# Which taps of a convolution go to which engine, in a fused state-space and attention kernel: the last chunk of four, the place of an eviction, and a clamp through PSUM

## The chip, the cores and the metric

The kernel runs on one core of one Trainium2 chip. The time is the device time of one execution in microseconds; times of several runs are given as median and range. A profile is one execution taken by the hardware profiler: start and end of the instructions of each engine, what released a waiting instruction, the DMA packets and the granted TensorE clock. The engines are called PE (TensorE), DVE (VectorE), ACT (ScalarE), POOL (GpSimd) and SP (SyncE, which here only issues DMAs).

## What is computed

Two layers on x of shape (2, 768, 64, 64). The change touches only the first, a two-dimensional Mamba block:

```python
x = hs @ in_proj_w.T                                  # 768 -> 1536 channels
xs = depthwise 3x3 convolution of x, + conv_b
xs = xs * sigmoid(xs)
dt, Bs, Cs = split(xs_seq @ x_proj_w.T, [R, R + DSTATE])
delta = softplus(dt @ dt_w + dt_b)
dA = exp(delta * A);  dBu = delta * u * Bs            # 4 states
states = associative scan of s = dA * s + dBu along the 4096 tokens
y = sum over states(states * Cs) + D * u
var = y.var(-1)
y = (y - mean) * rsqrt(var + 1e-5) * ln_g + ln_b      # over the 1536 channels
out = y @ out_proj_w.T                                # 1536 -> 768
```

A group norm stands before it and x is added to its output. The second layer (group norm, a token-statistics attention with two 768 x 768 products, residual) follows in the same program.

## The kernel before

**Tiles and steps.** The 2 x 4096 tokens are cut into 16 tiles of 512 tokens (8 image rows). The 1536 channels are 12 chunks of 128, so there are 192 pairs of tile and chunk, and the program is a sequence of steps g with three stages at different distances: the convolution runs ahead on chunk a = g + 15 (`AHEAD`, line 52), its input product on chunk n = g + 17, the scan works on chunk g, and the output product trails by 12 (`BEHIND`, line 53). Steps before g = 0 only fill this pipeline: 17 of them, after the group norm's statistics have been taken from a first reading of x. Every engine carries out its instructions in the order in which `step` (line 921) writes them; there is no reordering. Four chunks form a rhythm: the silu of chunks a-4 to a-1 runs in the steps with g % 4 = 1, followed by their x_proj products, and one third of a tile's output is evicted in steps with g % 4 = 0.

**The nine taps of the convolution.** `tap_act` (384) writes the centre tap into the PSUM tile acc on ACT. The other eight are divided by two tables, `DMA_TAPS` and `PE_TAPS` (lines 48 and 49, indexed by a % 4; `FILL_TAPS` for a < 15):
- A PE tap is a matmul with a diagonal matrix that adds into acc. ACT makes the diagonal (`diag`, 377); `taps_pe` (414) stands in the step before the chunk's own, behind that step's out_proj.
- A DMA tap is a scaled shifted copy made by ACT (`taps_act`, 393, tile tm), which DMAs with accumulation, issued by POOL, add up: `taps_dma_sum` (403) into the first tm, then `taps_dma` (408) into the chunk's result u.
- All remaining taps are DVE instructions (`taps_dve`, 423), one after the other on acc, the last one writing u.

For a chunk with three DMA taps (`late_tap`, line 1016) the second sum is issued in the chunk's own step and the final one is moved to the end of POOL's DMAs of that step; with two taps the final one stands ahead of the next chunk's first sum.

**One step on each engine.** DVE: the taps of chunk a, every fourth step the eviction of two output tiles (`out_evict`, 574: po times rs), then the scan's product s (506), the scan (508) and the product with C (515, tile da). In every twelfth step (g % 12 = 3) the layer norm's variance follows (`norm_rs2`, 551), from which ACT makes rs with Ln and Exp. POOL: `sum1` of the chunk before (493, tile ysum), `du` (485), then DMAs: tap sums, two y sums (501), and every fourth step the residual x (583). ACT: silu or softplus with their table loads, centre tap, eviction of in_proj (355), scaled copies for DMA taps, exps (480). PE: in_proj (342), norm sums, out_proj (558), PE taps, x_proj. SP issues the loads; behind g % 12 = 11 it broadcasts B and C of the next tile to all partitions (`load_bc`, 463).

**The fill.** In steps 8 to 15 of the fill the output weights are scaled by ln_g on ACT and their mean is subtracted on POOL (`out_weights_scale`, 274), behind the rest of the step; the table `ready_w` says which of the 12 blocks come in which step, one or two at a time. The in_proj results use one PSUM bank (psA), output products a pair of banks (psO) that the fill needs only for the weights' mean.

Of the kernel before, what the change touches and what calls it, by code (L numbers as in the profile page):

```python
# [7 lines left out]
F32 = mybir.dt.float32  # L8
AF = mybir.ActivationFunctionType
ALU = mybir.AluOpType  # L10
# [4 lines left out]
P = 128  # L15
# [7 lines left out]
KI = DI // P  # L23
# [11 lines left out]
NQ0 = NI * KI  # L35
# [9 lines left out]

DMA_TAPS = ((0, 2, 6), (0, 2), (0, 2, 6), (0, 2, 6))
PE_TAPS = ((), (1,), (), (1,))
FILL_TAPS = (0, 2)  # L50

AHEAD = 15
BEHIND = 12
# [13 lines left out]
def both_layers(  # L67
# [43 lines left out]
    def take():  # L111
        return slots.pop(0)
# [9 lines left out]
    def give_w(w):  # L122
        wst.append(w.rearrange("p k m -> p (k m)"))
    wk = ctx.enter_context(tc.tile_pool(name="l0wk", bufs=2))
    psA = ctx.enter_context(tc.tile_pool(name="l0_psa", bufs=1, space=PSUM))
# [3 lines left out]
    psO = ctx.enter_context(tc.tile_pool(name="l0_pso", bufs=1, space=PSUM))  # L129
# [121 lines left out]
    def out_weights_rows(wg, rows):  # L251
        gb = psO.tile([P, 2, 512], F32, tag="po", name="pgb")
        for k in range(KI):
            for j in range(KM // 2):
                nc.tensor.matmul(
                    gb[32 * j : 32 * j + 2, 0, :MG], pc[:, k, PC_G : PC_B + 1], wg[:, k, j * MG : (j + 1) * MG],
                    start=(k == 0), stop=(k == KI - 1),
                )
        for j in range(KM // 2):
            nc.scalar.copy(rows[32 * j : 32 * j + 2, :], gb[32 * j : 32 * j + 2, 0, :MG])  # L260

    def out_weights_mean(rows, wmean, pick):
        pb = psS.tile([P, 512], F32, tag="st", name="pbo")
        wm = psO.tile([P, 2, 512], F32, tag="po", name="pwm")
        for j in range(KM // 2):
            for e in range(2):
                m = 2 * j + e
                nc.tensor.matmul(pb[:, m : m + 1], rows[:, e * P : (e + 1) * P], pick[:, j, P : P + 1], start=True, stop=True)
            nc.tensor.matmul(wm[:, j // 2, j % 2 * MG : (j % 2 + 1) * MG], pick[:, j, :P], rows, start=True, stop=True)
        nc.scalar.copy(wmean[:, : 2 * MG], wm[:, 0, :])  # L270
        nc.scalar.copy(wmean[:, 2 * MG :], wm[:, 1, :MG])
        nc.scalar.copy(bias_o, pb[:, :KM])

    def out_weights_scale(wg, wmean, k):
        nc.scalar.activation(wg[:, k, :], wg[:, k, :], AF.Copy, scale=pc[:, k, PC_G : PC_G + 1])
        nc.gpsimd.tensor_sub(wg[:, k, :], wg[:, k, :], wmean)

    def out_weights_store(wg, k):
        nc.sync.dma_start(
# [6 lines left out]
    def where(n):  # L286
        i, c = divmod(n, KI)
        return i, c, i // NT, i % NT
# [53 lines left out]
    def in_proj(n):  # L342
        i, c, b, t = where(n)
        nn = TL if t < NT - 1 or b + 1 < NB else TL - W
        w = wis.pop(n)
        pa = psA.tile([P, 512], F32, tag="psa", name=f"pa{n}")
        for k in range(KM):
            nc.tensor.matmul(pa[:, :nn], w[:, k, :], xts[i, k][:, :nn], start=(k == 0), stop=(k == KM - 1))  # L348
        pas[n] = pa
        give_w(w)  # L350
        if c == KI - 1:
            for k in range(KM):
                give(xts.pop((i, k)))
# [15 lines left out]


    def dma_taps(a):
        return DMA_TAPS[a % 4] if a >= AHEAD else FILL_TAPS

    def pe_taps(a):
        return PE_TAPS[a % 4] if a >= AHEAD else ()

    def diag(a):
        c = a % KI
# [14 lines left out]
    def taps_act(a):  # L393
        xs, c = xs_bufs[a % 2], a % KI
        tms[a] = (tm_bufs[a % 2], tm_bufs[2], tm_bufs[3 + a % 2]) if a >= AHEAD else (take(), take())
        for tm, j in zip(tms[a], dma_taps(a)):
            dy, dx = divmod(j, 3)
            nc.scalar.activation(  # L398
                tm.rearrange("p (h w) -> p h w", w=W), xs[:, dy : dy + TR, dx : dx + W], AF.Copy,
                scale=pc[:, c, PC_W + j : PC_W + j + 1],  # L400
            )

    def taps_dma_sum(a, q):
        nc.gpsimd.dma_start(tms[a][0], tms[a][q], accum_op=ALU.add)  # L404
        if a < AHEAD:
            give(tms[a][q])

    def taps_dma(a):
        tm = tms.pop(a)[0]
        nc.gpsimd.dma_start(us[a], tm, accum_op=ALU.add)  # L410
        if a < AHEAD:
            give(tm)
# [7 lines left out]
                skip_group_check=True,  # L420
            )

    def taps_dve(a):
        c = a % KI
        taps = [j for j in range(9) if j != 4 and j not in pe_taps(a) + dma_taps(a)]
        xs, acc = xs_bufs[a % 2], accs.pop(a).rearrange("p (h w) -> p h w", w=W)
        u = take()
        us[a] = u
        for j in taps:
            dy, dx = divmod(j, 3)  # L430
            dst = u.rearrange("p (h w) -> p h w", w=W) if j == taps[-1] else acc
            nc.vector.scalar_tensor_tensor(  # L432
                dst, xs[:, dy : dy + TR, dx : dx + W], pc[:, c, PC_W + j : PC_W + j + 1], acc, ALU.mult, ALU.add
            )

    def silu(a):
        nc.scalar.activation(us[a], us[a], AF.Silu, bias=pc[:, a % KI, PC_CB : PC_CB + 1])
# [15 lines left out]
    def x_sum(i):  # L453
        px = psX.tile([P, 512], F32, tag="px", name=f"pxs{i}")
        nc.tensor.matmul(px[:XM, :], xsum, pxs["halves"], start=True, stop=True)
        give(pxs.pop("halves"))
        pxs["sum"] = px
# [43 lines left out]
    def y_dma(g, n):  # L501
        nc.gpsimd.dma_start(us[g], ysums(g, n), accum_op=ALU.add)  # L502
# [46 lines left out]
        return pm, mu2  # L549

    def norm_rs2(i, pm, mu2):
        nc.vector.scalar_tensor_tensor(mu2, mu2, -1.0, pm[:, 1, :], ALU.mult, ALU.add)
        nc.vector.tensor_scalar_max(mu2, mu2, 0.0)
        nc.scalar.activation(rs, mu2, AF.Ln, bias=eps_c)
        nc.scalar.activation(rs, rs, AF.Exp, scale=-0.5)

# [17 lines left out]
    def out_evict(g):  # L574

        po = pos[0]
        i, r = (g - 1 - BEHIND) // KI, (g - 1) % KI
        for e in range(2):
            xr = take()
            nc.vector.tensor_mul(xr, po[:, e, :], rs)  # L580
            xrs[i, 2 * (r // 4) + e] = xr
# [60 lines left out]
    def norm_x1(b, j, k):  # L642
        nc.scalar.activation(
            x1s[b, j, k], x1s[b, j, k], AF.Identity, bias=bias1[b][:, k : k + 1], scale=scale1[b][:, k : k + 1]
        )
# [248 lines left out]
    with tc.manual_schedule():  # L894
# [26 lines left out]
        def step(g, prep=None):  # L921
            a, n = g + AHEAD, g + AHEAD + 2
            v = n
# [29 lines left out]
                norms[g][0][1]()  # L953
            if xd_now:
                x_sum(g // KI + 1)
            if 0 <= a < NQ0:
                taps_dve(a)
            if BEHIND < g <= NQ0 + BEHIND and (g - BEHIND) % 4 == 0:
                out_evict(g)
            for q in by_step[v - 1] if 0 < v <= len(by_step) else ():  # L960
                gn_piece(1, q)
            if BEHIND + 2 < g and (g - BEHIND) % 4 == 2:
# [33 lines left out]
            elif n < NQ0 + N_TAIL:  # L996
# [3 lines left out]
                    load_x1(0, d[1] + 1, k)  # L1000
                for k in {3: [0], 4: [1], 5: [2, 3, 4, 5]}.get(d[2], []):
                    norm_x1(0, d[1] + 1, k)
            if 0 <= a + 1 < NQ0:
                taps_act(a + 1)
            if 0 <= g - 3 < NQ0:
                square(g - 3)
# [9 lines left out]
            late_tap = 0 <= a < NQ0 and len(dma_taps(a)) > 2  # L1016
# [3 lines left out]
                y_dma(g - 1, 0)  # L1020
            if 0 <= g - 2 < NQ0:
                y_dma(g - 2, 1)
            if 0 <= a < NQ0 and not late_tap:
                taps_dma(a)
            if 0 <= a + 1 < NQ0:
                taps_dma_sum(a + 1, 1)
            if late_tap:
                taps_dma(a)
# [48 lines left out]
        with tc.tile_pool(name="l0st", bufs=1, side="right") as sp:  # L1077
            wg = sp.tile([P, KI, DM], F32, name="wg")
            rows = sp.tile([P, MG], F32, name="gb_rows")
            nc.vector.memset(rows, 0.0)  # L1080
            wmean = sp.tile([P, DM], F32, name="wmean")
            pick = sp.tile([P, KM // 2, P + 1], F32, name="pick")
            nc.sync.dma_start(pick, pick_in)

            first = -AHEAD - 2
            ready_w = {8: (0,), 9: (1, 2), 10: (3,), 11: (4, 5), 12: (6, 7), 13: (8, 9), 14: (10,), 15: (11,)}
            prep = {7: lambda: out_weights_rows(wg, rows), 8: lambda: out_weights_mean(rows, wmean, pick)}
            for v in range(AHEAD + 1):
                if 2 <= v < 6:
                    out_weights_load(wg, 3 * (v - 2))  # L1090
                step(first + v, prep.get(v))
                if v == 0:
                    nc.scalar.activation(neg_a, pc[:, :, PC_A : PC_A + NS], AF.Exp)
                    nc.scalar.mul(neg_a, neg_a, -1.0)
                for k in ready_w.get(v, ()):
                    out_weights_scale(wg, wmean, k)
                for k in ready_w.get(v - 1, ()):
                    out_weights_store(wg, k)
            for k in ready_w[AHEAD]:
                out_weights_store(wg, k)  # L1100
# [10 lines left out]
        for g in range(-1, NQ0 + 2):  # L1111
            step(g)
# [163 lines left out]
```

## Time and profile before

| What | Value |
|---|---|
| median of 3 runs | 3868.43 us (3867.46 to 3874.68) |
| profiled execution | 3868.68 us |
| its span, first to last instruction | 3866.9 us |
| granted TensorE clock, mean | 0.981 |
| busy over the span | PE 94%, DVE 72%, ACT 64%, POOL 43% |
| first scan starts at | 213.9 us |
| last scan starts at | 2756.8 us |
| busy between 2761 us and the end (1105.6 us) | PE 1074.6, DVE 226.1 us |

A profile line of a group names the code line, the engine, the operation and the tiles it writes and reads (out<-in), the shape and the count; behind the bar stand busy time in us, mean ns of one, and the idle time of the engine just before, with what ended it. A line in order of time has the start in us from the beginning of the span, the length in us, the instruction, a count where several in a row were merged, and in brackets the engine's idle time before it and the releaser. A wait for several semaphores is put down to the one that came last. Idle time costs nothing on an engine that does not hold others up. A DMA issue appears under the engine that issues it; it lands later.

### The profile page before, as it was taken

To read this page: it belongs to the slowest core of one execution; us is meant where nothing else is said; L and a number is where in the kernel's file an instruction comes from. 1 tells how busy PE (TensorE), PEld (TensorE's weight loads), DVE (VectorE), ACT (ScalarE), POOL (GpSimd) and SP (SyncE) were. 2 spreads that over 40 slices of the span, in tenths; PEclk is the share of its full clock that TensorE was granted. 3 is DMA by queue.
4 is the path that set the end of the run, shared out by engine and by line. 5 is a ranking of instruction groups with operands and counts; after the bars stand their busy time and mean duration, and the time that the engine had idled before them with its cause. 6 is when DMAs were issued, how large, how long until landed. Compare 5 with 4: busy or idle time off the path is not lost.

```text
span 3866.9 us, 32976 instructions
## 1 busy us (share of the span) xinstructions
PE 3631.4 (94%) x9794; PEld 1511.2 (39%) x9794; DVE 2783.4 (72%) x2331; ACT 2480.1 (64%) x4691; POOL 1655.0 (43%) x1512
## 2 busy tenths in 40 slices
PE   5867999999999999999999999999999999998999
PEld 3422333333333333333433333333344444444444
DVE  8589999999999999999999999987400620005311
ACT  2677888888898888988889888886423511123000
POOL 0445555565555555555655556554200011111222
PEclk9888999999999999999999999999999999999999
DMA  9777898898988988899888998876544144442455
GB/s 351 197 165 151 174 204 181 196 207 189 205 183 196 211 185 203 183 206 207 186 197 182 208 203 185 201 175 163 147 122 136 62 149 150 153 143 79 143 180 155
DMA packets 325795, 687.52 MB, mean 178 GB/s; under 512 B 37824, under 2 KB 45952, under 8 KB 321520
## 3 DMA queue, kind: packets, MB, share of 16 engines
q0 software_dynamic: 143568, 261.42, 40.2%
q1 hardware_dynamic: 182048, 424.00, 33.5%
q8 instruction: 78, 1.28, 0.1%
q14 instruction: 101, 0.83, 0.1%
HBM read 393.77 MB, written 55.31 MB: 116 GB/s over the span
## 4 chain that ended last, share of the span: by engine, by line
DVE 40%; PE 32%; ACT 8%; issue 6%; DMA 6%; POOL 4%; SPq 0%; DVEq 0%; POOLq 0%; ACTq 0%
DVE s L508 16%; PE mm L682 13%; PE mm L655 9%; DVE acc L432 8%; DVE da L515 8%; DVE s L506 6%; PE po L568 3%; DMA tm<-tm 2%; PE pa L348 2%; DMA u<-tm 2%; PE pq L655 2%; DMA u<-ysum 2%; POOL ysum L495 1%; ACT da L483 1%; POOL du L487 1%
## 5 line engine op out<-in xcount | busy, mean ns | idle before, releaser
L568 PE MATMUL po<-u,w 128*128 128x512 f32 x2304 | 1051.2, 606 | 68.4 <-DVE u L580 68.0
L348 PE MATMUL pa<-u,w 128*128 128x512 f32 (+1 forms) x2304 | 1042.9, 603 | 6.1 <-ACT carry L363 5.6
L508 DVE TENSOR_TENSOR_SCAN s<-da,s 128x2052 f32<-128x2052 f32 x192 | 851.1, 4433 | 19.5 <-DVE s L506 0.5
L568 PEld LDWEIGHTS po<-u,w 128*128 128x128 f32 x2304 | 432.8, 192 | 674.9 <-issue 571.6
L348 PEld LDWEIGHTS pa<-u,w 128*128 128x128 f32 x2304 | 431.4, 192 | 600.7 <-issue 535.5
L495 POOL TENSOR_TENSOR ysum<-da 128x1024 f32<-128x1024 f32 x192 | 394.6, 2055 | 540.3 <-DVE da L515 514.0
L432 DVE SCALAR_TENSOR_TENSOR acc<-xs,pc,acc 128x512 f32<-128x512 f32 x738 | 556.4, 754 | 73.1 <-ACT acc L386 44.7
L506 DVE TENSOR_TENSOR s<-du,bc 128x2048 f32<-128x2048 f32 x192 | 438.8, 2286 | 75.0 <-POOL du L487 71.7
L677 POOL TENSOR_TENSOR w<-w,at 128x768 f32<-128x768 f32 x96 | 141.1, 1471 | 815.0 <-DMA w<-woutP 565.4
L483 ACT ACTIVATE da<-dl,neg_a 128x512 f32<-128x512 f32 x768 | 489.7, 713 | 0.0
L404 POOL DMA_DIRECT2D tm<-tm x310 | 270.7, 874 | 478.8 <-ACT tm L398 417.5
L515 DVE TENSOR_TENSOR da<-s,bc 128x2048 f32<-128x2048 f32 x192 | 440.0, 2292 | 6.3
L502 POOL DMA_DIRECT2D u<-ysum x384 | 389.4, 1303 | 3.4 <-issue 2.3
L398 ACT ACTIVATE tm<-xs,pc 128x512 f32<-128x512 f32 x487 | 317.8, 718 | 5.5 <-DMA tm<-tm 4.2
L682 PE MATMUL mm<-u,w 128*128 128x512 f32 x684 | 320.6, 596 | 0.0
L691 DVE TENSOR_TENSOR u<-mm,u 128x512 f32<-128x512 f32 x59 | 40.8, 692 | 336.3 <-PE mm L682 336.3
L487 POOL TENSOR_TENSOR du<-dl,u 128x512 f32<-128x512 f32 x192 | 256.9, 1338 | 0.0
L410 POOL DMA_DIRECT2D u<-tm x177 | 217.5, 1229 | 84.1 <-DMA tm<-tm 54.6
L386 ACT ACTIVATE acc<-xs,pc 128x512 f32<-128x512 f32 x192 | 132.5, 690 | 187.7 <-DVE u L432 185.0
L682 PE MATMUL mm<-v,w 128*128 128x512 f32 x468 | 225.7, 593 | 0.0
L655 PE MATMUL mm<-u,w 128*128 128x512 f32 x456 | 214.4, 594 | 0.0
L682 PEld LDWEIGHTS mm<-u,w 128*128 128x128 f32 x684 | 129.3, 191 | 167.8 <-issue 167.8
(211 smaller groups left out, 4065.6 us busy)
## 6 DMA issues: line engine op xcount, KB each, us to landing
u<-ysum POOLq DMA_DIRECT2D x384, 256.0 KB, 5.9
tm<-tm POOLq DMA_DIRECT2D x310, 256.0 KB, 4.7
w<-in_wP SPq DMA_DIRECT2D x192, 384.0 KB, 4.3
w<-wo_dr SPq DMA_DIRECT2D x192, 384.0 KB, 5.2
u<-x SPq DMA_DIRECT2D x278, 256.0 KB, 3.9
u<-tm POOLq DMA_DIRECT2D x177, 256.0 KB, 5.9
w<-qkvP SPq DMA_DIRECT2D x96, 384.0 KB, 3.2
w<-woutP SPq DMA_DIRECT2D x96, 384.0 KB, 3.8
```

The costliest lines, as they stand in the source:

```text
L348: nc.tensor.matmul(pa[:, :nn], w[:, k, :], xts[i, k][:, :nn], start=(k == 0), stop=(k == KM - 1))
L398: nc.scalar.activation(tm.rearrange("p (h w) -> p h w", w=W), xs[:, dy : dy + TR, dx : dx + W], AF.Copy, scale=pc[:, c, PC_W + j : PC_W + ...
L432: nc.vector.scalar_tensor_tensor(dst, xs[:, dy : dy + TR, dx : dx + W], pc[:, c, PC_W + j : PC_W + j + 1], acc, ALU.mult, ALU.add)
L483: nc.scalar.activation(das[g % 2][:, n, 1:], deltas[g], AF.Exp, scale=neg_a[:, c, n : n + 1])
L495: nc.gpsimd.tensor_add(ysum[:, 0 : 2 + g % 2 : 1 + g % 2, :], da[:, 0:2, 1:], da[:, 2:4, 1:])
L502: nc.gpsimd.dma_start(us[g], ysums(g, n), accum_op=ALU.add)
L506: nc.vector.tensor_mul(s[:, :, 1:], dus.pop(g).unsqueeze(1).to_broadcast([P, NS, TL]), bc[:, :NS, :])
L508: nc.vector.tensor_tensor_scan(sf, das[g % 2].rearrange("p n l -> p (n l)"), sf, 0.0, ALU.mult, ALU.add)
L515: nc.vector.tensor_mul(das[g % 2][:, :, 1:], s[:, :, 1:], bc[:, NS:, :])
L568: nc.tensor.matmul(po[:, e, :], w[:, kk, e * P : (e + 1) * P], us[i * KI + k], start=(k == 0), stop=(k == KI - 1))
L655: nc.tensor.matmul(pa, w[:, k, :], x1s[b, j, k], start=(k == 0), stop=(k == KM - 1))
L682: nc.tensor.matmul(po, w[:, k, :], w1s[b, k, j], start=(k == 0), stop=(k == KM - 1))
```

## The change

- The tap tables of the steady part: the two-DMA-tap chunk moves from a % 4 = 1 to a % 4 = 3, and so do the PE taps, which become taps 1 and 7 of that chunk instead of tap 1 of two chunks.
- The fill gets tables of its own: chunks 3, 7 and 11 have no DMA tap and one PE tap; the others keep two DMA taps. Calls that would do nothing are left out.
- The eviction of the output runs behind the first DVE tap of its step, through a function handed to `taps_dve`.
- The variance is written back into the PSUM tile of the means, and the clamp at zero reads it from there into SBUF.
- In the fill, where two weight blocks come in one step, the second subtraction is on DVE.
- In the fill, the in_proj results of chunks 13 and 15 use the output product's PSUM tile.

```diff
-DMA_TAPS = ((0, 2, 6), (0, 2), (0, 2, 6), (0, 2, 6))
-PE_TAPS = ((), (1,), (), (1,))
-FILL_TAPS = (0, 2)
+DMA_TAPS = ((0, 2, 6), (0, 2, 6), (0, 2, 6), (0, 2))
+PE_TAPS = ((), (), (), (1, 7))
+FILL_DMA_TAPS = ((0, 2), (0, 2), (0, 2), ())
+FILL_PE_TAPS = ((), (), (), (1,))
...
-    def out_weights_scale(wg, wmean, k):
+    def out_weights_scale(wg, wmean, k, engine):
         nc.scalar.activation(wg[:, k, :], wg[:, k, :], AF.Copy, scale=pc[:, k, PC_G : PC_G + 1])
-        nc.gpsimd.tensor_sub(wg[:, k, :], wg[:, k, :], wmean)
+        engine.tensor_sub(wg[:, k, :], wg[:, k, :], wmean)
...
-        pa = psA.tile([P, 512], F32, tag="psa", name=f"pa{n}")
+        if KI <= n < AHEAD + 2 and n % 2:
+            pa = psO.tile([P, 2, 512], F32, tag="po", name=f"pa{n}")[:, 0, :]
+        else:
+            pa = psA.tile([P, 512], F32, tag="psa", name=f"pa{n}")
...
-    def taps_dve(a):
+    def taps_dve(a, after_first):
...
                 dst, xs[:, dy : dy + TR, dx : dx + W], pc[:, c, PC_W + j : PC_W + j + 1], acc, ALU.mult, ALU.add
             )
+            if j == taps[0]:
+                after_first()
...
-        nc.vector.scalar_tensor_tensor(mu2, mu2, -1.0, pm[:, 1, :], ALU.mult, ALU.add)
-        nc.vector.tensor_scalar_max(mu2, mu2, 0.0)
+        nc.vector.scalar_tensor_tensor(pm[:, 0, :], mu2, -1.0, pm[:, 1, :], ALU.mult, ALU.add)
+        nc.vector.tensor_scalar_max(mu2, pm[:, 0, :], 0.0)
...
+            evict = (lambda: out_evict(g)) if BEHIND < g <= NQ0 + BEHIND and (g - BEHIND) % 4 == 0 else (lambda: None)
             if 0 <= a < NQ0:
-                taps_dve(a)
-            if BEHIND < g <= NQ0 + BEHIND and (g - BEHIND) % 4 == 0:
-                out_evict(g)
+                taps_dve(a, evict)
+            else:
+                evict()
...
-            if 0 <= a < NQ0 and not late_tap:
+            if 0 <= a < NQ0 and dma_taps(a) and not late_tap:
                 taps_dma(a)
-            if 0 <= a + 1 < NQ0:
+            if 0 <= a + 1 < NQ0 and dma_taps(a + 1):
                 taps_dma_sum(a + 1, 1)
...
-                for k in ready_w.get(v, ()):
-                    out_weights_scale(wg, wmean, k)
+                for k, engine in zip(ready_w.get(v, ()), (nc.gpsimd, nc.vector)):
+                    out_weights_scale(wg, wmean, k, engine)
```

More of the change, by code (lines that the diff above doesn't have):

```diff
@@ L371, in dma_taps @@
     def dma_taps(a):
-        return DMA_TAPS[a % 4] if a >= AHEAD else FILL_TAPS
+        return (DMA_TAPS if a >= AHEAD else FILL_DMA_TAPS)[a % 4]
     def pe_taps(a):
-        return PE_TAPS[a % 4] if a >= AHEAD else ()
+        return (PE_TAPS if a >= AHEAD else FILL_PE_TAPS)[a % 4]
     def diag(a):
@@ L1022, in step @@
                 y_dma(g - 2, 1)
-            if 0 <= a < NQ0 and not late_tap:
+            if 0 <= a < NQ0 and dma_taps(a) and not late_tap:
                 taps_dma(a)
-            if 0 <= a + 1 < NQ0:
+            if 0 <= a + 1 < NQ0 and dma_taps(a + 1):
                 taps_dma_sum(a + 1, 1)
```

## The prediction

> **What bounds the kernel now.** I read the busy time by stretch first, then the waits, then the order of time of single steps. A step g handles conv chunk a = g+15, scan chunk g and a quarter of an output chunk; twelve steps are one tile of 512 tokens. The stretch view over steps 12 to 177 (columns: length, then busy us and count of PE, PEld, DVE, ACT, POOL; granted clock; DMA share, GB/s):
>
> ```profile
> 367.00:2590.00 2223.00, 2138.67 (x5625) 851.04 (x5624) 2147.50 (x1412) 1910.76 (x3591) 1297.00 (x1204) 0.99 0.89 195
> ```
>
> DVE is busy 97%, PE 96%: two near-limits. The order of time settles which one leads. Scan starts in quiet steps are 12.89 us apart, and that is DVE's own list without a gap: five taps 3.8, s 2.29, scan 4.43, da 2.29. A step with eviction takes 13.29, with the norm as well 15.59. A quiet tile is therefore 9 x 12.89 + 2 x 13.29 + 15.59 = 158.2 us. Between the scans of g=16 (433.27) and g=172 (2512.46) lie 13 tiles, 159.9 us each: 1.75 us of each are DVE waits. PE's list over four steps, from the chain of waits, is 8 x 5.35 + 2 x 1.06 + 2 x 1.00 + 1.72 + 1.87 = 50.5 us, against 51.96 for DVE: PE follows with 1.5 us to spare. After g=191 (2757 us) PE alone sets the pace; whatever is saved before shifts that part.
>
> From the view of waits (us in total, times, longest):
>
> ```profile
> DVE s L506 <- POOL du L487: 71.7, 36, 5.5
> PE po L568 <- DVE u L580: 68.0, 36, 6.6
> POOL u L410 <- DMA tm<-tm: 54.6, 19, 5.7
> ACT u L437 <- DMA u<-tm: 54.3, 15, 5.4
> ```
>
> 47.3 of the 71.7 lie after step 177, where no taps are left (mostly 3.4 us a step): untouched. The rest belongs to the third and fourth rows.
>
> **Part 1: the order of taps.** Over four steady chunks the counts stay: 11 DMA taps, 2 PE taps, 19 DVE taps. What moves is which chunk has three DMA taps and so issues its last sum at the end of POOL's queue. Before, that is so for the last chunk (a%4=3), although the next step's silu needs it first. Step 96 to 97, in order of time:
>
> ```profile
> 1493.02 0.86 POOL L404 DMA_DIRECT2D tm<-tm  x1
> 1495.99 0.85 POOL L404 DMA_DIRECT2D tm<-tm  x1 [0.33 <-ACT tm L398]
> 1501.45 0.85 POOL L410 DMA_DIRECT2D u<-tm  x1 [4.61 <-DMA tm<-tm]
> 1501.99 2.10 POOL L588 DMA_DIRECT2D u<-x  x2
> 1503.60 2.52 POOL L495 TENSOR_TENSOR ysum<-da 128x1024 f32<-128x1024 f32 x1
> 1505.57 1.77 POOL L487 TENSOR_TENSOR du<-dl,u 128x512 f32<-128x512 f32 x1
> 1507.38 2.29 DVE L506 TENSOR_TENSOR s<-du,bc 128x2048 f32<-128x2048 f32 x1 [0.50 <-POOL du L487]
> 1507.59 0.72 ACT L437 ACTIVATE u<-u,pc 128x512 f32<-128x512 f32 x1 [2.99 <-DMA u<-tm]
> ```
>
> The reader sees two victims of one late sum: POOL stands 4.6 us, pushing residual, ysum and du until DVE waits for du; ACT stands 3 us at the last silu and is late in the next step. It happens once per tile, in g%12=1, when the broadcast of B and C fills the DMA queues. Afterwards the first sum of that chunk is already issued in the step before (11 us earlier here) and the last goes out behind the two y sums, at about 1495, six us sooner; the usual 5.9 us to land meet a silu at 1504.6. The late place passes to a%4=1, whose silu is three steps off; POOL's queue behind it holds no residual. In those 13 tiles steps g%12=1 exceed 12.89 by 9.9 us in sum (the group-norm step 121 left out), g%12=2 by 6.8. Some is other DMA trouble; I take three quarters: **-12.5**. The same stall in g=13 costs 3.0 of DVE wait and in g=1 3.9: **-7**. ACT gives 0.72 for a tap and takes 0.40 for a diagonal in the silu step, and the reverse two steps later; its result for the taps is ready 3 to 10 us ahead, so nothing.
>
> Two PE taps now stand ahead of DVE's first tap in a%4=3: one more pair of matmuls, 0.86, at the end of PE's queue. PE's taps end 0.04 to 2.9 us before DVE's start there. But PE does the same work between two evictions, and part 2 lets it go on earlier: no cost; if that fails, 0.8 in every fourth step.
>
> **Part 2: eviction behind the first tap.** PE's next group waits for it 1 to 2 us; with three taps fewer ahead (2.4 us) that wait goes. PE is not the bound, so this only repays the second PE tap. On DVE, a dependent tap starts 0.79 after the one before, the independent eviction 0.67 after: pulling tap and tap apart saves 0.12 in 41 steps: **-4.9**. ACT's next acc moves 1.2 back, into its reserve above. Outputs of out_proj are there 0.9 us or more before even the first tap; rs is not always.
>
> **Part 3: clamp through PSUM, and the wait it meets.** Rows by form (us, mean ns), then one norm in order of time:
>
> ```profile
> L580 DVE TENSOR_TENSOR u<-po,rs 128x512 f32<-128x512 f32 x92 | 59.0, 682 | 2.9 <-ACT rs L555 2.9
> L553 DVE TENSOR_SCALAR mu<-mu 128x512 f32<-128x512 f32 x16 | 24.0, 1502 | 0.6
> L552 DVE SCALAR_TENSOR_TENSOR mu<-mu,pm 128x512 f32<-128x512 f32 x16 | 10.9, 683 | 46.0 <-ACT mu L548 45.8
> ```
>
> ```profile
> 1542.43 2.00 POOL L495 TENSOR_TENSOR ysum<-da 128x1024 f32<-128x1024 f32 x1 [3.31 <-DVE da L515]
> 1542.98 1.73 DVE L553 TENSOR_SCALAR mu<-mu 128x512 f32<-128x512 f32 x1
> 1544.63 2.33 DVE L432 SCALAR_TENSOR_TENSOR acc<-xs,pc,acc 128x512 f32<-128x512 f32 x3
> 1545.50 0.63 ACT L555 ACTIVATE rs<-rs 128x512 f32<-128x512 f32 x1
> 1547.66 1.28 DVE L580 TENSOR_TENSOR u<-po,rs 128x512 f32<-128x512 f32 x2
> ```
>
> The clamp ends 0.285 us after POOL's ysum ends, in every norm but the last; that one, with POOL idle, takes 0.426. So it waits for POOL. The Trainium skill speaks against the change here: VectorE: DVE Perf Modes, the cycle table and "Why PSUM operands drop a tier", gives an fp32 tensor_scalar two elements a cycle in SBUF only and more start-up from PSUM, (58+256)/0.96 = 327 ns against (120+512)/0.96 = 658. By the rule 16 clamps cost 16 x 0.33 = +5.3 us; by the rows, with 0.68 for an operation that reads PSUM (the first and third), the 14 under taps give 21.8 - 14 x 0.68 = -12.3, and the one at 2662 us -1.1. I take the rows: the rule does not count POOL. No row writes this tile to PSUM, but acc (754 ns, PSUM) and u (748, SBUF) are alike; bounds for the clamp 0.43 and 1.73.
>
> Most of it is handed back. From the end of the clamp to rs takes Ln and Exp 1.45 us (here 1544.71 to 1546.15; in the norm at 2662, without taps, DVE stands exactly 1.45). Before, four taps cover it. Afterwards one tap covers 0.6, and the eviction waits about 0.86, with three taps, s and the scan behind it: 14 x 0.86 = **+12**. Part 3 with this wait: -12.3 - 1.1 + 12 = **-1.4**. If the tap covered nothing it would be 14 x 1.45 = 20 instead of 12.
>
> **Part 4: the fill (before 214 us).** Chunks 3, 7, 11 lose both DMA taps, get one on PE and seven on DVE (before six). The silu of chunk 3 stood 5.0 us for DMA, that of chunk 11 4.7:
>
> ```profile
> 110.78 0.72 ACT L437 ACTIVATE u<-u,pc 128x512 f32<-128x512 f32 x1 [5.02 <-DMA u<-u]
> 159.95 3.91 DVE L432 SCALAR_TENSOR_TENSOR acc<-xs,pc,acc 128x512 f32<-128x512 f32 x5
> 164.47 1.75 ACT L275 ACTIVATE wg<-wg,pc 128x768 f32<-128x768 f32 x2
> ```
>
> Against that, every second weight subtraction goes from POOL (2.2 us) to DVE (about 0.95, as 128x768 against the 2.29 of 2048 columns), where it stands in order before the next chunk's taps and waits for ACT's scaling at the step's end. The last two rows show it: the taps at 159.95 will wait for the scaling that ends at 166.2, then the subtraction, then start at 167.2; the next chunk by another 4.5, and ACT's acc, the eviction of in_proj and so PE behind them. The other two places lie under silu. So about -6 at chunk 3, +0.9 for a PE tap, and at chunk 11 the 4.7 and the spare bank for chunks 13 and 15 against some 10: even to -3 overall. I take **-2.5**, bounds -9 and +8.
>
> **Sum**, against the profiled execution's 3868.68 (span 3866.9; the median, 3868.43, is the same within 0.01%): -12.5 - 7 - 4.9 - 1.4 - 2.5 = -28.3, some **3840 us**.
>
> **Rivals.** *Only the stalls of the first tiles go* (chance 0.15): the steady sums land late anyway, because the broadcast fills the queues at 1495 as at 1493, and the eviction waits the full 1.45 for rs. That is -7 - 4.9 - 2.5 and for part 3 14 x 1.45 - 12.3 - 1.1 = +6.9: 3861. For it: one such sum took 8 us to land there; against: the sum has six us more. *All waits go and the start gains its full 9* (0.20): -16.7 - 7 - 4.9 - 1.4 - 9 = -39: 3830. For it: each of these waits is traced to the one late sum. *DVE's queue loses the fill* (0.10, slower): the wait for ACT's scaling, the subtraction behind it, is hidden at none of its four places. Taps then start at the end of the scaling + 0.95 instead of at 139.79, 159.95, 166.82 and 172.64: 9.3 + 7.2 + 4.7 + 5.1 = +26, while the steady sums stay late and nothing is won at the start; with -4.9 and -1.4 it gives 3888. It decides once the fill loses more than the steady part saves. Against it: the first and the last place precede four silus that take ACT 5 us with their table loads anyway. That the change doesn't do what it says I exclude: the two programs' lists of instructions differ as described.
>
> **Chances.** Main case 0.55, own range 3830 to 3852. 0.2% (7.7 us) is about what a measurement here tells from no change. Faster: 0.55 + 0.20 + a third of the first rival's 0.15 = 0.80; within: the other two thirds, 0.10; slower 0.10. The range, 3820 to 3862, goes from the second rival less its unknown landings to the end of the first.
>
> **What would show it.** L437's wait for u<-tm at g%12=1 gone and steps there near 12.89; the clamp near 0.68; a wait of rs of 0.8 before each norm's eviction; PE's wait for the eviction near nothing; first scan some us before 213.9. Wrong if DVE waits for PE's acc in every fourth step, or the first scan starts later.

## The result and the profile after

| | before | after |
|---|---|---|
| median of 6 runs, us | 3869.18 (3866.22 to 3874.68) | 3844.76 (3839.27 to 3847.85) |
| profiled execution, us | 3868.68 | 3841.76 |
| its span, us | 3866.9 | 3840.0 |
| first scan starts at | 213.93 | 211.75 |
| scan of g=16 | 433.27 | 424.89 |
| scan of g=172 | 2512.46 | 2487.67 |
| last scan (g=191) | 2756.82 | 2729.73 |

The ratio of the times is 0.9934, with a 95% interval of 0.9921 to 0.9947. The change saves 24.4 us by the medians and 26.9 us between the two profiled executions, where 28.3 were predicted. The scan starts tell in which stretch the time is won: 2.2 us before the first scan, 6.2 up to g=16, 16.4 in the 13 tiles up to g=172, and 2.3 up to the last scan. Behind that, nothing.

First the busy time by stretch of the changed kernel over nearly the same steps as before (length, then busy us and count of PE, PEld, DVE, ACT, POOL; granted clock; DMA share, GB/s):

```profile
367.00:2570.00 2203.00, 2138.69 (x5628) 852.91 (x5627) 2130.17 (x1407) 1906.36 (x3595) 1289.58 (x1201) 0.99 0.90 197
```

The stretch is 20 us shorter. PE's 2138.69 us equal those of before to a few hundredths and now fill 97% of it; the granted clock is the same 0.99. DVE's busy time is 17 us less: 14 clamps that are about 0.9 shorter give some 12 of it, and the ends of the stretch cut five instructions fewer. Its idle time, 75.5 us before, is 72.8. So most of the waits that went must have been replaced, and the waits of DVE in this stretch (us in total, times, longest) show by what:

```profile
DVE s L512 <- POOL du L493: 11.7, 11, 3.4
DVE u L586 <- ACT rs L561: 11.0, 14, 0.8
DVE pm L558 <- ACT mu L554: 3.5, 2, 2.5
```

The wait for du was 25.4 us in 20 times here before: 13.7 are gone. The wait for rs is new, 14 times 0.79 us, and takes back what the clamps gave.

The waits of the changed kernel over its whole span (us in total, times, longest):

```profile
DVE s L512 <- POOL du L493: 53.9, 26, 4.8
...
PE po L574 <- DVE u L586: 33.3, 22, 5.1
POOL tm L408 <- DMA tm<-tm: 14.6, 15, 2.0
...
DVE u L586 <- ACT rs L561: 13.9, 16, 1.5
...
ACT u L443 <- DMA u<-tm: 12.7, 13, 1.6
```

The first row lost 17.8 us. The row of the late sum that stood third before, POOL waiting at the final tap sum for 54.6 us, has no successor: at its line (414 now) POOL waits for no DMA any more. ACT's wait at the silu fell from 54.3 to 12.7 us but is not gone: in nearly every tile the sum still lands about 1 us late. PE's wait for the eviction is halved. The wait of the eviction for rs, 2.9 us before, is now 13.9, as predicted. There is no row of DVE waiting in every fourth step for PE's taps.

Steps 96 to 97 in order of time:

```profile
1475.12 1.76 POOL L508 DMA_DIRECT2D u<-ysum  x2
1476.49 1.28 POOL L414 DMA_DIRECT2D u<-tm  x1
1479.16 0.85 POOL L408 DMA_DIRECT2D tm<-tm  x1 [1.39 <-ACT tm L402]
1479.69 2.09 POOL L594 DMA_DIRECT2D u<-x  x2
1485.57 2.00 POOL L501 TENSOR_TENSOR ysum<-da 128x1024 f32<-128x1024 f32 x1 [3.79 <-DMA u<-ysum]
1487.48 0.72 ACT L443 ACTIVATE u<-u,pc 128x512 f32<-128x512 f32 x1 [0.98 <-DMA u<-tm]
1487.54 1.28 POOL L493 TENSOR_TENSOR du<-dl,u 128x512 f32<-128x512 f32 x1
1488.85 2.29 DVE L512 TENSOR_TENSOR s<-du,bc 128x2048 f32<-128x2048 f32 x1
```

The final sum (L414) now goes out right behind the two y sums and POOL does not stand at it. It is issued 11 us before the silu reads it and still lands 0.98 us late: the DMAs took 10 us here, not the 5.9 I had taken. But the residual (L594), ysum and du no longer stand behind it; du ends at 1488.8, and DVE's s starts there without a wait.

The groups by form (us, mean ns of one, idle before with its releaser), and below them the norm at g=99 in order of time:

```profile
L586 DVE TENSOR_TENSOR u<-po,rs 128x512 f32<-128x512 f32 x92 | 59.0, 683 | 13.9 <-ACT rs L561 13.9
...
L559 DVE TENSOR_SCALAR mu<-pm 128x512 f32<-128x512 f32 x16 | 11.1, 692 | 0.5
L558 DVE SCALAR_TENSOR_TENSOR pm<-mu,pm 128x512 f32<-128x512 f32 x16 | 11.0, 690 | 46.7 <-ACT mu L554 46.7
```

```profile
1523.70 0.69 DVE L558 SCALAR_TENSOR_TENSOR pm<-mu,pm 128x512 f32<-128x512 f32 x1
1523.86 2.00 POOL L501 TENSOR_TENSOR ysum<-da 128x1024 f32<-128x1024 f32 x1 [1.57 <-DVE da L521]
1524.42 0.69 DVE L559 TENSOR_SCALAR mu<-pm 128x512 f32<-128x512 f32 x1
1525.03 0.75 DVE L436 SCALAR_TENSOR_TENSOR acc<-xs,pc,acc 128x512 f32<-128x512 f32 x1
1525.90 0.63 ACT L561 ACTIVATE rs<-rs 128x512 f32<-128x512 f32 x1
1526.56 1.29 DVE L586 TENSOR_TENSOR u<-po,rs 128x512 f32<-128x512 f32 x2 [0.79 <-ACT rs L561]
1527.77 1.54 DVE L436 SCALAR_TENSOR_TENSOR acc<-xs,pc,acc 128x512 f32<-128x512 f32 x2
```

The clamp now takes 0.69 us in the middle of POOL's ysum, which runs from 1523.86 to 1525.86; before, it lasted until that had ended. Writing the variance into PSUM costs 690 ns instead of 683. Then DVE carries out one tap and stands 0.79 us for rs, with three ready taps behind the eviction in its queue (two of them in the last line).

The fill, around the weight subtractions:

```profile
159.40 2.08 POOL L277 TENSOR_TENSOR wg<-wg,wmean 128x768 f32<-128x768 f32 x1
160.18 2.13 DVE L277 TENSOR_TENSOR wg<-wg,wmean 128x768 f32<-128x768 f32 x1 [7.91 <-ACT wg L276]
162.23 3.91 DVE L436 SCALAR_TENSOR_TENSOR acc<-xs,pc,acc 128x512 f32<-128x512 f32 x5
167.02 0.69 ACT L390 ACTIVATE acc<-xs,pc 128x512 f32<-128x512 f32 x1 [6.58 <-DVE u L436]
167.76 2.08 PE L422 MATMUL acc<-xs,dg 128*128 128x512 f32 x2 [7.13 <-ACT acc L390]
```

DVE stands 7.9 us for ACT's scaling, and the subtraction then takes 2.13 us instead of the 0.95 that I had estimated: it ends 0.83 us after POOL's own subtraction, which started 0.78 us earlier. The taps begin only at 162.23. ACT's next centre tap waits 6.6 us for them and PE 7.1. On the other side, no silu before the first scan waits for a tap sum any more.

### The profile page after: what moved, and what is told of

It is laid out like the page before. It is cut to its first block, busy times and chain, and to the rows that moved or that the text cites. A ratio compares the mean times of both kernels' runs of the same rounds, so it can differ in the third digit from the quotient of the medians.

```text
span 3840.0 us, 32997 instructions
## 1 busy us (share of the span) xinstructions
PE 3633.3 (95%) x9802; PEld 1514.7 (39%) x9802; DVE 2776.7 (72%) x2338; ACT 2470.1 (64%) x4688; POOL 1638.2 (43%) x1501
## 4 chain that ended last, share of the span: by engine, by line
DVE 39%; PE 37%; ACT 7%; issue 7%; DMA 6%; POOL 3%; SPq 0%; DVEq 0%; POOLq 0%; ACTq 0%
DVE s L514 15%; PE mm L688 13%; PE mm L661 9%; DVE acc L436 8%; DVE da L521 6%; DVE s L512 6%; PE po L574 4%; PE pa L352 4%; DMA u<-ysum 3%; PE pq L661 2%; DVE u L586 1%; DVE u L436 1%; DMA u<-tm 1%; ACT tm L402 1%; POOL du L493 1%
## 5 line engine op out<-in xcount | busy, mean ns | idle before, releaser
L574 PE MATMUL po<-u,w 128*128 128x512 f32 x2304 | 1038.7, 600 | 33.5 <-DVE u L586 33.3
L501 POOL TENSOR_TENSOR ysum<-da 128x1024 f32<-128x1024 f32 x192 | 384.5, 2002 | 576.6 <-DVE da L521 446.3
L436 DVE SCALAR_TENSOR_TENSOR acc<-xs,pc,acc 128x512 f32<-128x512 f32 x741 | 558.2, 753 | 39.3 <-PE acc L422 12.8
L512 DVE TENSOR_TENSOR s<-du,bc 128x2048 f32<-128x2048 f32 x192 | 438.8, 2286 | 54.6 <-POOL du L493 53.9
L508 POOL DMA_DIRECT2D u<-ysum x384 | 377.7, 1245 | 3.5 <-issue 2.4
L493 POOL TENSOR_TENSOR du<-dl,u 128x512 f32<-128x512 f32 x192 | 244.2, 1272 | 0.0
L414 POOL DMA_DIRECT2D u<-tm x177 | 205.2, 1159 | 54.1 <-issue 35.7
```

What stands on the lines that cost most here:

```text
L436: nc.vector.scalar_tensor_tensor(dst, xs[:, dy : dy + TR, dx : dx + W], pc[:, c, PC_W + j : PC_W + j + 1], acc, ALU.mult, ALU.add)
L501: nc.gpsimd.tensor_add(ysum[:, 0 : 2 + g % 2 : 1 + g % 2, :], da[:, 0:2, 1:], da[:, 2:4, 1:])
L512: nc.vector.tensor_mul(s[:, :, 1:], dus.pop(g).unsqueeze(1).to_broadcast([P, NS, TL]), bc[:, :NS, :])
L574: nc.tensor.matmul(po[:, e, :], w[:, kk, e * P : (e + 1) * P], us[i * KI + k], start=(k == 0), stop=(k == KI - 1))
```

## The experiments

**Which part brings the gain: the tables alone.** The kernel before with the two tables of the steady part and nothing else:

```diff
-DMA_TAPS = ((0, 2, 6), (0, 2), (0, 2, 6), (0, 2, 6))
-PE_TAPS = ((), (1,), (), (1,))
+DMA_TAPS = ((0, 2, 6), (0, 2, 6), (0, 2, 6), (0, 2))
+PE_TAPS = ((), (), (), (1, 7))
```

> The kernel before with only the two steady tap tables changed (eviction behind all taps, clamp in SBUF, the fill as before). Theory of the late sum: the waits for du in steps g%12=1 and 2 go, about 12 us in the 13 tiles, and 7 us in g=1 and g=13; evicting steps stay at 13.29 us, norm steps at 15.59, the first scan at 214: about 3850. Rival, TensorE: the second PE tap needs the earlier eviction, so DVE waits for PE's acc by some 0.5 to 0.9 us in most steps with g%4=0, 20 to 35 us: 3865 to 3885.

Measured: 3850.40 us (3848.40 to 3853.45), 0.9947 (0.9933 to 0.9962) of the kernel before on the same chip (3871.94). The first scan starts at 214.00, as before; the period of g=1 is 14.26 instead of 18.27; a tile takes 159.10 instead of 159.94, and its eviction and norm steps are the old 13.29 and 15.59. In the view of waits between 367 and 2577 us, PE stands at the eviction no less than before, where it was 57.0 us in 34 times (columns: us in total, times, longest):

```profile
PE po L568 <- DVE u L580: 61.3, 37, 3.6
```

So it is the place of the late sum that holds DVE: the gain lies in the steps in which DVE waited for du behind that sum (the PE taps move with it and were not moved alone). The tables alone bring most of the gain: 17.9 us of 26.9 between the profiled executions (span 3849.0), 21.5 of 24.4 by the medians. The spans fit the steps: 6.8 up to g=16 (433.27 to 426.50), most of it in g=1 and g=13, and 13 x 0.84 = 10.9 in the tiles are 17.7 of the 17.9. PE keeps its reserve: it still stands for the eviction, and no wait of DVE for PE's taps appears, even with the eviction where it was. The rival in which PE takes over falls. (One wait of DVE for the means, 2.4 us in g=123, does come from PE; see the 13 tiles below.)

**The eviction behind all taps again.** The changed kernel, with only the eviction put back:

```diff
-                taps_dve(a, evict)
-            else:
-                evict()
+                taps_dve(a, lambda: None)
+            evict()
```

> The changed kernel with the eviction behind all taps again. Theory: evicting steps go from 13.16 back to 13.29 us, but norm steps from 15.30 to about 14.54, since rs is covered by four taps: -0.5 us a tile, in all some 7 us faster than the changed kernel, about 3838. Rival, TensorE: with two PE taps and the late eviction DVE waits for PE's acc at g%4=0, 10 us or more slower than the changed kernel.

Measured: 3835.07 us (3833.23 to 3836.99), 0.9907 (0.9892 to 0.9922). That is faster than the changed kernel by 9.7 us in the medians and by 7.3 in the spans (3832.7 against 3840.0). The norm step falls from 15.30 to 14.55 and the eviction step goes back from 13.16 to 13.29: per tile -0.75 + 2 x 0.13 = -0.49, times 13 is 6.4 us. (This profile also holds 2.7 us more than the changed kernel's in the one step before the scan of g=121, explained with the 13 tiles below, so the spans understate the difference.) Moving the eviction is therefore a loss for the kernel as it is: it saves 0.13 in the quiet steps and gives back 0.75 in each norm step, because the eviction then waits for rs ahead of taps that are ready. PE's shorter wait for the eviction buys nothing, since PE does not lead here.

**The clamp in SBUF again.** The changed kernel with the two lines of the variance as before:

```diff
-        nc.vector.scalar_tensor_tensor(pm[:, 0, :], mu2, -1.0, pm[:, 1, :], ALU.mult, ALU.add)
-        nc.vector.tensor_scalar_max(mu2, pm[:, 0, :], 0.0)
+        nc.vector.scalar_tensor_tensor(mu2, mu2, -1.0, pm[:, 1, :], ALU.mult, ALU.add)
+        nc.vector.tensor_scalar_max(mu2, mu2, 0.0)
```

> The changed kernel with variance and clamp in SBUF again. Theory of the POOL wait: the clamp is 1.73 us again and ends 0.285 us after POOL's ysum, the eviction waits its 0.79 as now; norm steps 15.30 to 16.35 us, in all 12 to 13 us slower than the changed kernel, about 3857. Rival, the rule of the perf modes alone: the clamp is 0.33 us shorter in SBUF, 5 us faster, about 3840.

Measured: 3860.77 us (3857.39 to 3865.53), 0.9972 (0.9960 to 0.9985): 16 us slower than the changed kernel. Its norm in order of time:

```profile
1531.69 2.00 POOL L501 TENSOR_TENSOR ysum<-da 128x1024 f32<-128x1024 f32 x1 [1.56 <-DVE da L521]
1532.24 1.73 DVE L559 TENSOR_SCALAR mu<-mu 128x512 f32<-128x512 f32 x1
...
1535.42 1.29 DVE L586 TENSOR_TENSOR u<-po,rs 128x512 f32<-128x512 f32 x2 [0.79 <-ACT rs L561]
```

The clamp takes 1.73 us again and ends 0.28 after POOL's ysum (1531.69 + 2.00 = 1533.69). The wait for rs stays at 0.79, since one tap stands between clamp and eviction in both. So the two parts add up: the norm step is 16.34 instead of 15.30. The rival, that the rule of the Trainium skill's "VectorE: DVE Perf Modes" holds and the clamp is quicker from SBUF, falls beside a running POOL. A tile takes 1.30 us more, of which the norm step explains 1.04. Of the remaining 0.26 x 13 = 3.4 us, 2.9 lie in the single step before the scan of g=121 (16.99 against 14.11 us), and not at the clamp; the 13 tiles below show what happens there.

**The subtractions of the fill.** Three kernels stand side by side: the change (one of each two on DVE), all on POOL, and all on DVE. In the last, the single blocks' subtractions are on DVE as well, not only those of the pairs.

```diff
-                for k, engine in zip(ready_w.get(v, ()), (nc.gpsimd, nc.vector)):
+                for k, engine in zip(ready_w.get(v, ()), (nc.gpsimd, nc.gpsimd)):
```

> The changed kernel with all weight subtractions of the fill on POOL. Theory: DVE no longer stands 6.8 + 7.9 + 2.7 + 3.4 us for ACT's scaling and 2.1 us in each subtraction; the taps of chunks 10 and 11 and with them ACT and PE come earlier, first scan at about 203 instead of 211.8, 3836. Rival: POOL's four more subtractions of 2.1 us hold up its DMA sums, the silu of chunks 8 to 11 waits for them, and the first scan stays within 2 us of 211.8: 3845.

Measured: 3831.17 us (3827.94 to 3832.53), 0.9896 (0.9881 to 0.9911): 13.6 us faster than the changed kernel. The first scan starts at 199.42 instead of 211.75, more than I expected. The four subtractions on DVE thus cost 12.3 us.

```diff
-                for k, engine in zip(ready_w.get(v, ()), (nc.gpsimd, nc.vector)):
+                for k, engine in zip(ready_w.get(v, ()), (nc.vector, nc.vector)):
```

> The changed kernel with both subtractions of a pair on DVE, none of these on POOL. Theory of the shared port: DVE's 2.1 us in the changed kernel are 0.95 of its own and the rest waiting for POOL's own subtraction to end; with POOL free of it a subtraction on DVE takes 0.95 us. First scan near 211. Rival: the shape or the tiles make it 2.1 us on DVE by itself, and all eight take that.

Measured in one run: 3854.66 us, first scan at 218.08 (expected about 211). The place in the queue costs more than I thought: with twelve subtractions and their waits for ACT's scaling in DVE's order instead of four, the fill is 6.3 us longer. But the length of one subtraction settles the other question. The group of this kernel, and a pair in order of time:

```profile
L277 DVE TENSOR_TENSOR wg<-wg,wmean 128x768 f32<-128x768 f32 x12 | 11.1, 956 | 34.9 <-ACT wg L276 34.9
```

```profile
164.20 1.83 DVE L277 TENSOR_TENSOR wg<-wg,wmean 128x768 f32<-128x768 f32 x2 [4.66 <-ACT wg L276]
```

And the same line in the changed kernel:

```profile
L277 POOL TENSOR_TENSOR wg<-wg,wmean 128x768 f32<-128x768 f32 x8 | 16.2, 2023 | 10.9 <-ACT wg L276 10.9
L277 DVE TENSOR_TENSOR wg<-wg,wmean 128x768 f32<-128x768 f32 x4 | 8.3, 2077 | 20.8 <-ACT wg L276 20.8
```

Alone on DVE a subtraction takes 956 ns, and two of them 1.83 us. Beside POOL's it takes 2077 ns, because it waits for POOL's to end: the two that were meant to run side by side run one after the other. POOL's keep their 2.0 us.

**The tables of the fill.** The kernel with all subtractions on POOL, and the fill's taps divided as before:

```diff
-FILL_DMA_TAPS = ((0, 2), (0, 2), (0, 2), ())
-FILL_PE_TAPS = ((), (), (), (1,))
+FILL_DMA_TAPS = ((0, 2), (0, 2), (0, 2), (0, 2))
+FILL_PE_TAPS = ((), (), (), ())
```

> As the run with all subtractions on POOL (first scan 199.4), but every chunk of the fill has two DMA taps and no PE tap. Theory: the last silus of chunks 3 and 11 stand some 5 us each for their DMA sums again, and the first scan comes at about 208: some 8 us slower than 3831, 3839. Rival: those stalls are beside the chain of in_proj on PE and its eviction; first scan at 199 to 202, time within 3 us of 3831.

Measured: 3845.52 us (3842.28 to 3847.60), 0.9927 (0.9911 to 0.9944), with the first scan at 211.34: 14.4 us and 11.9 us later than with the new tables. The stalls of the silu of chunks 3 and 11 are back, and one at chunk 2 just before, which took 3.37 us in the kernel before and which the prediction did not count (ACT in order of time):

```profile
105.04 0.72 ACT L443 ACTIVATE u<-u,pc 128x512 f32<-128x512 f32 x1 [2.82 <-DMA u<-u]
111.11 0.72 ACT L443 ACTIVATE u<-u,pc 128x512 f32<-128x512 f32 x1 [5.35 <-DMA u<-u]
...
184.21 0.72 ACT L443 ACTIVATE u<-u,pc 128x512 f32<-128x512 f32 x1 [4.65 <-DMA u<-u]
```

2.82 + 5.35 + 4.65 = 12.8 us of stalls stand against the 11.9 us by which the first scan comes later.

**The spare PSUM bank.** The same kernel with in_proj in its one bank throughout:

```diff
-        if KI <= n < AHEAD + 2 and n % 2:
-            pa = psO.tile([P, 2, 512], F32, tag="po", name=f"pa{n}")[:, 0, :]
-        else:
-            pa = psA.tile([P, 512], F32, tag="psa", name=f"pa{n}")
+        pa = psA.tile([P, 512], F32, tag="psa", name=f"pa{n}")
```

> As the run with all subtractions on POOL, but in_proj of chunks 13 and 15 use the one bank of the others again. Theory: PE waits for ACT's eviction before these products, behind silu in one of them; first scan about 3 us later, at 202, about 3834. Rival: ACT is the chain of the fill in these steps and the bank changes nothing: first scan within 1 us of 199.4.

Measured: 3831.74 us (3828.06 to 3838.38), 0.9894 (0.9879 to 0.9909), first scan at 199.53 against 199.42. Beside the new tables the bank brings nothing, and the rival is right here. PE does wait for ACT's eviction without it (2.11 and 1.80 us before two in_proj products), but the first scan doesn't come later for it. With the old tables it is otherwise. The fills of the tables-alone kernel (first scan 214.00) and of the kernel with the fill's old tables (211.34) differ in nothing but the bank. Without it PE stands 1.02, 0.84 and 0.90 us for ACT's eviction behind 165 us; with it none of these waits is left, and the first scan comes 2.7 us earlier.

**The better version.** All subtractions on POOL, and in the norm step the eviction behind the second tap, elsewhere behind the first:

```diff
-    def taps_dve(a, after_first):
+    def taps_dve(a, after, at):
...
-            if j == taps[0]:
-                after_first()
+            if j == taps[at]:
+                after()
...
-                taps_dve(a, evict)
+                taps_dve(a, evict, int(g % KI == 4))
...
-                for k, engine in zip(ready_w.get(v, ()), (nc.gpsimd, nc.vector)):
+                for k, engine in zip(ready_w.get(v, ()), (nc.gpsimd, nc.gpsimd)):
```

> All weight subtractions of the fill on POOL, and in the norm's steps (g%12=4) the eviction behind the second tap instead of the first; in the other evicting steps it stays behind the first. Theory of the cover: one more tap hides 0.79 of the 1.45 us to rs, so the wait before the norm's eviction falls from 0.79 to under 0.1, norm steps go from 15.30 to about 14.5 us and the others stay at 13.16: 14 x 0.8 = 11 us faster than the run with subtractions on POOL (3831), about 3820. Rival: the eviction 0.8 us later lets PE's acc arrive late at the next g%4=0; then DVE waits there and the time stays at 3828 or more.

Measured: 3819.19 us (3817.17 to 3822.87), 0.9861 (0.9846 to 0.9875): 54.8 us faster than the kernel before on the same chip (3873.97), and 25.6 less than the changed kernel's median. Its norm:

```profile
1504.97 0.69 DVE L559 TENSOR_SCALAR mu<-pm 128x512 f32<-128x512 f32 x1
1505.58 1.54 DVE L436 SCALAR_TENSOR_TENSOR acc<-xs,pc,acc 128x512 f32<-128x512 f32 x2
1507.11 1.29 DVE L586 TENSOR_TENSOR u<-po,rs 128x512 f32<-128x512 f32 x2
1508.32 0.74 DVE L436 SCALAR_TENSOR_TENSOR acc<-xs,pc,acc 128x512 f32<-128x512 f32 x1
```

Two taps cover Ln and Exp, no bracket with a wait is left, and the eviction still lies between two taps. The norm step takes 14.51, the eviction step 13.16. Both losses of the change are gone and its gains are kept.

## Why the prediction was right, and where its terms were not

The forecast and its place hold: DVE was held by one late sum per tile, and the sum's move, not a cheaper instruction, brings the time. (The measured -13.7 us of DVE's wait for du and the -14.3 of step lengths are two readings of the same thing.) By its own steps, us of gain (-) or loss (+), with the measured value from scan starts and step lengths:

| Term | predicted | measured |
|---|---|---|
| stalls of g%12=1 and 2, 13 tiles | -12.5 | -14.3 |
| the same in g=1 and g=13 | -7 | -4.0 - 2.7 = -6.7 |
| eviction between two taps | 0.12 a step, -4.9 in all | 0.13 a step; 26 steps of the 13 tiles: -3.1 |
| clamp, per norm | 1.56 (21.8 / 14) to 0.68: -0.88 | norm step with the clamp in SBUF 16.34, with PSUM 15.30: -1.04 |
| wait for rs, per norm | +0.86 | +0.79 |
| PE taps moved to a%4=3 | 0 | +2.5 once, at the norm of g=123 |
| fill | -2.5 | -2.2 |

**The tap order** was right in its mechanism, with one row read too favourably: I took 5.9 us for the sum to land, it took 10, and ACT still waits 1 us in most tiles. It does not matter, because POOL no longer stands at that sum, and POOL's stand was what reached DVE.

**PE's second diagonal tap** costs nothing in the steps for which the price was named, as argued. But the reason I gave, that the earlier eviction pays for it, was not needed: the tables alone, with the eviction in its old place, show no wait of DVE for PE's taps either. What I put at nothing and was not nothing is one wait per execution, at the change from the first image to the second; it stands with the 13 tiles below.

**The clamp.** The row was the right guide, and the rule alone the wrong one. The operation that reads PSUM took 692 ns against the 658 that the rule gives; from SBUF, the rule's 327 was never what the trace showed under POOL's ysum. The Trainium skill's page "SBUF — State Buffer", section "SBUF: two separate sides", states the mechanism that I had read off the clamp's rows but left out of the fill's sum: VectorE and GpSimd share one pair of SBUF ports, and whichever starts first, a GpSimd operation or a VectorE operation in a two-port mode or with two SBUF inputs (these only against a GpSimd operation that reads SBUF), keeps the pair for its whole instruction. The clamps and the subtractions of these runs agree: they end 0.28 and 0.83 us after POOL's instruction and are not merely slower.

**The wait for rs** was sized right, and so was the conclusion that it hands most of the clamp's gain back. What I did not draw from it is that both parts could be had without it, by one tap more ahead of the eviction.

**The fill is the step that failed.** Its sum was nearly met, -2.5 against -2.2, but that is luck: two terms were wrong and cancel. I had put the tables at about 6 us for chunk 3, and 4.7 and the spare bank at chunk 11 against "some 10" for the subtractions. The runs give, one change at a time, by the start of the first scan: bank with the old tables 214.00 to 211.34, -2.7; tables 211.34 to 199.42, -11.9; subtractions 199.42 to 211.75, +12.3. The three add up to -2.3, against -2.2 measured. Taken out after the tables, the bank is worth only 0.1, so its gain doesn't add to theirs. The estimate of 0.95 for a subtraction on DVE came from an operation with two SBUF inputs that never lies under a tensor operation of POOL (none of the 192 does); beside POOL's subtraction it is 2.1. The longer duration is 4 x (2.08 - 0.96) = 4.5 of the 12.3 us; the rest I put to the place in DVE's queue, behind waits for ACT's scaling of up to 7.9 us; no run separates the two. Kernels whose fill is the same start their first scan up to 1.5 us apart (211.24 to 212.75), so the bank's 2.7 is the least certain of these numbers, though the vanished waits of PE, 2.8 us in sum, bear it out.

**The 13 tiles** gained 16.4 us by -14.3 at the stalls, -3.1 at two evictions per tile, -1.1 at the norm steps, and +2.2 in the rest. The norm steps would have given -0.29 x 13 = -3.8, but the norm step that ends at the scan of g=124 took 17.86 us, with a wait of 2.5 for the means from ACT. ACT had them late because PE was late, and the reason lies one step earlier. Before, one of the PE taps stood in step 121, and PE waited 1.90 us there for its acc. The new tables have none there, so PE reaches the product pz of step 122 earlier. The PSUM buffers of pz also serve the group norm's statistics (pg_y), which DVE copies to gs_y at its own place, 4.35 us into the step, in both kernels. PE in order of time, before:

```profile
1846.84 1.13 PE L471 MATMUL pz<-xd,dt_w 48*128 48x512 f32 x4
1847.90 5.42 PE L348 MATMUL pa<-u,w 128*128 128x512 f32 x12
```

and after:

```profile
1825.79 2.08 PE L477 MATMUL pz<-xd,dt_w 48*128 48x512 f32 x4 [4.23 <-DVE gs_y L193]
1827.80 6.85 PE L352 MATMUL pa<-u,w 128*128 128x512 f32 x12
```

The head start is lost in a wait of 4.23 us. From 1825.8 to 1828.0 the granted clock is 0.50, where it is 1.00 in the same place before, and the two products take 8.9 us instead of 6.5: 2.4 us later come the means. All nine profiles with the new tables have this wait of DVE (2.0 to 3.4 us); the one of the kernel before, whose longest wait for the means in this stretch is 0.9, has not.

A second cost of the tables is missing from the profile of the changed kernel only by luck. In the step before the scan of g=121, DVE carries out five tiny operations on the statistics of the second layer's group norm, 0.17 us each. Before, POOL stood at the late sum in that step; now it is free, and its ysum and du start among these operations. In the kernel with the tables alone:

```profile
1806.03 2.00 POOL L495 TENSOR_TENSOR ysum<-da 128x1024 f32<-128x1024 f32 x1 [4.51 <-DVE da L515]
1806.20 1.85 DVE L623 TENSOR_SCALAR mv<-mv 128x12 f32<-128x12 f32 x1
1808.00 1.26 POOL L487 TENSOR_TENSOR du<-dl,u 128x512 f32<-128x512 f32 x1
1808.09 1.20 DVE L625 TENSOR_TENSOR msq<-mv,stats 128x6 f32<-128x6 f32 x1
1809.32 0.17 DVE L626 TENSOR_TENSOR msq<-msq 128x6 f32<-128x6 f32 x1
```

Two of the five wait here until POOL's instruction has ended. One or two do so in eight of the nine profiles with the new tables, where this step is 1.8 to 2.9 us longer; in the changed kernel's own, ysum started just as the last of the five ended. That profiled execution lies 3.0 us below the median of its kernel. This may be a part of the reason, but the other executions have no trace to show it.

## What to carry to other kernels

Where several engines' instructions stand in fixed order, look first for the one queue in which a late transfer makes everything behind it late, and move the transfer, not the work: here two tables alone brought two thirds of the gain between the profiled executions and nearly nine tenths by the medians. Then look at what the freed engines meet next: here POOL met DVE's small operations, and PE a shared PSUM buffer. Do not put an instruction that waits for another engine ahead of work that is ready; count the ready instructions that must come first to cover that wait (one tap of 0.75 us, begun as the clamp ended, did not cover 1.45; two of 1.54 together did). Before an operation is divided between DVE and POOL, look whether both read two SBUF operands, as these subtractions do: then the two may take turns, and the division wins nothing while its place in the queue still costs.

## What the hardware showed that was not expected

I had expected two subtractions, one on DVE and one on POOL, to run side by side. They take turns. The subtraction of 128x768 takes 956 ns alone and 2077 on average beside POOL's (2.13 us where it began 0.78 us after one of 2.08), and ends about 0.83 us after POOL's. The clamp, one SBUF input of fp32, behaves the same way: it ends 0.28 us after POOL's ysum and takes 1.73 us, while from PSUM it takes 0.69 in the middle of it. So do the tiny operations at g=121: 0.17 us alone, up to 2.0 us beside ysum, ended 0.02 to 0.03 us after it. They and the clamp have no tile in common with ysum. All three kinds end at POOL's end plus their own time alone (0.956, 0.426, 0.17) less 0.13 to 0.14 us. DVE's convolution taps, with one input in PSUM and one in SBUF, don't wait: 620 of the 741 that write acc in the changed kernel lie under a tensor operation of POOL, and they take 753 ns, as the other 121 do. POOL's side is hardly touched: 2023 ns on average over its eight, four of them beside DVE's, and 2076 in the kernel where POOL does all twelve.
